# Two layers of cross-attention on one core: VectorE's and ScalarE's order written out by hand

## The chip, the core and the metric

The kernel runs on one NeuronCore of a Trainium2 chip. The metric is the device time of one execution in microseconds (us). TensorE (PE) multiplies matrices and transposes, VectorE (DVE) and ScalarE (ACT) work on what it leaves in PSUM, GpSimd (POOL) adds in SBUF and issues DMAs of results, SyncE (SP) issues the loads. All arithmetic is in float32.

## The reference, cut to what matters

Two layers follow one another. For each of 8 images there are 100 queries of 640 channels (20 heads of 32 channels), 77 text tokens and 645 image tokens of 1024 channels.

```
layer 0:  q = x Wq;  k, v = text Wk, text Wv;  k_ip, v_ip = ip Wk_ip, ip Wv_ip
          out = softmax(q k / sqrt(32)) v + softmax(q k_ip / sqrt(32)) v_ip      (each head)
          x1  = out Wo + bo + x
layer 1:  the same with its own weights, but
          sem  = (softmax over text of q k_text, all 640 channels) text . ip / sqrt(32)
          ip probabilities = softmax(scores_ip + 0.5 sem) * mask of the query
          result = out Wout + bout + x1
```

A layer of an image is called a unit u (0 to 15; layer 1 from 8 on), four heads of a unit are a chunk c (0 to 4), so there are 80 chunks in all, listed in ORDER.

## The kernel before, in words

**First part (to about 200 us).** Queries of layer 0, keys and values of the text and of the last five image tokens are made and written to DRAM.

**Second part (200 to 2070 us).** Two streams of work are interleaved by hand.

The first stream makes keys and values of the image tokens for two images at once (a pair of units; pair_tasks, and for the last pair two_chunks and fifth_chunk). Matrices are multiplied in the manner of Strassen, with seven products in place of eight: `seven` (L179) gives seven steps, first, sixth, second, seventh, fifth, fourth, third. Each step is one product on PE into a PSUM bank (psv_a to psv_e for values, psk_a to psk_e for keys, psvk_a to psvk_e for the last pair) and then an instruction that takes it out: a copy by ACT (L193, L202) or an addition by DVE (L198, L208, L213, L219, L224). There are two banks for it (ps_pj). Sums of tokens that the products need come from DVE (token_sums, L231; third_sum, L527; L725 and L726 in the last pair), sums of weights too (weight_sums, L127, four additions L134 to L137; `asked` spreads them as tasks, in the first pair two of the four run on POOL). `last_k` is the plain product for the fifth group of keys.

The second stream is the attention of the chunks. For a chunk, `scores` (L934) with part 0 makes scores with 512 keys and with part 1 those with 210 keys. Both parts use one PSUM tile, sc, of four banks, one for each head. DVE takes the maxima (L953; in layer 1 L960, with the semantic scores added), ACT the exponentials (L968), DVE the text maxima and differences (L974 to L980), ACT their exponentials (L983, L984), DVE the factors (L985 to L991), and then the probabilities are scaled: 512 columns by ACT (L997), the rest by DVE (L1001, L1005). What can wait is put in the list `later` in portions, and `emit(n)` takes n of them. A portion marked True has to be out before the score tile is used again (free_scores, L928).

One chunk later, `transposes` (L1021) turns the probabilities on PE in six groups, pspt, four heads each; DVE copies groups 0, 1, 3 and 4 (L1037), ACT groups 2 and 5 (L1035). `values` (L1040) multiplies with the values (pv) and DVE copies the result (hs, L1056). Two PSUM banks (ps_pt) are shared by pspt, pv and by all small work of a chunk: out_piece (pso L858, taken out by DVE at L863), q_piece (psq, by ACT at L881), and for layer 1's semantic scores sem_text (L831, ACT L833), sem_logits (L805, DVE L810, ACT L811, DVE L812 and L813), sem_transpose (L818, ACT L820) and sem_scores (L840, ACT L841).

**The order of the work.** `production` lists the first stream's tasks with a cost each (0 for sums and loads) and `spread` gives each a place between chunks. The loop over ORDER at the end goes through a chunk so: score product part 0; tasks and small work; transposes 0 and 1 of the chunk before; tasks and small work; transposes 2 and 3; score product part 1; tasks and small work; transposes 4 and 5; tasks and small work; the values of the chunk before. `between` (L1240) runs the tasks that are due and the small work, `apart` sees to it that there is a product between two things that use the same banks where one is to be had, and `next_task` (L1220) runs one task and, if it had a cost, emits one portion. `small_work` (L1148) says which small work a chunk has.

The loop stands in a block in which PE runs its instructions in the order in which the program gives them:

```
with tc.manual_schedule(engines={mybir.EngineType.PE}):
```

The order on the other engines is chosen by the compiler's scheduler, from the dependences and its own estimate of times.

Of the kernel before, what the change touches and what calls it, by code (L numbers as in the profile page):

```python
# [9 lines left out]
F32 = mybir.dt.float32  # L10
AF = mybir.ActivationFunctionType
ALU = mybir.AluOpType
AX = mybir.AxisListType

P = 128
# [29 lines left out]
def two_layer_xattn(  # L45
# [654 lines left out]
    def last_visits(visits):  # L700

        xs, lists = {}, []
        for i, (j, tasks_of) in enumerate(visits):

            def begin(i=i):
                if i == 0:
                    xs.update(places[LAST])
                elif i + 2 < len(visits):
                    xs[i + 2] = load_x(LAST, visits[i + 2][0])

            lists.append([(0.0, begin)] + tasks_of(j, xs, i))
        return lists

    def two_chunks(r, j, xs, at):
        n0, n1 = BLOCKS[j]
        n = n1 - n0
        sums, o, made, late = {}, {}, {}, []

        def begin():
            t = spool.tile([P, 3, HK, 2, NX], F32, tag="s", name=f"sl_{r}_{j}")  # L720
            a11, a12, a21, a22 = quarters(xs[at], n)
            s1, s2, s4 = (t[:, i, :, 0, :n] for i in range(3))
            sums.update(token_sums(a11, a12, a21, a22, s1, s2, None, s4))
            sums[7] = a21
            late.append(lambda: nc.vector.tensor_tensor(a21, a11, a21, ALU.subtract))  # L725
            late.append(lambda: nc.vector.tensor_tensor(s4, a12, s2, ALU.subtract))  # L726
            o[0] = opool.tile([P, 2, 2, P + NX], F32, tag="made", name=f"vko_{r}_{j}")

        def product(ps, which, go_on):
            for k in range(HK):  # L730
                nc.tensor.matmul(
                    ps[:, :P], lhsT=sums[which][:, k, :P], rhs=W["v", WHICH[which]][:, k, r * P : (r + 1) * P],
                    start=(k == 0 and not go_on), stop=(k == HK - 1), skip_group_check=True,
                )
            for k in range(HK):
                nc.tensor.matmul(
                    ps[:, P : P + n], lhsT=W["k", WHICH[which]][:, k, r * P : (r + 1) * P], rhs=sums[which][:, k, :],
                    start=False, stop=(k == HK - 1), skip_group_check=True,
                )

        def step(i):
            if i == 0:
                made[0] = seven(
                    f"psvk_{r}_{j}", product, tuple(o[0][:, h, m, : P + n] for h in range(2) for m in range(2))
                )
            made[0][i]()
            if i < 6:
                return
            for h, u in enumerate(LAST):
                nc.gpsimd.dma_start(  # L750
                    k_d[u][:, :4, n0:n1].rearrange("p (m r) n -> p r m n", r=2)[:, r], o[0][:, h, :, P : P + n]
                )
                nc.gpsimd.dma_start(
                    v_d[u][j * P : (j + 1) * P, : 4 * P].rearrange("p (m r n) -> p r m n", m=2, r=2)[:, r],
                    o[0][:, h, :, :P],
                )

        steps = [(1.8, lambda i=i: step(i)) for i in range(7)]
        sums_ = [(0.0, lambda i=i: late[i]()) for i in range(2)]
        return [(0.0, begin)] + steps[:1] + sums_[:1] + steps[1:4] + sums_[1:] + steps[4:]  # L760

    def fifth_chunk(kinds, j, xs, at):
        n0, n1 = BLOCKS[j]
        tasks = []
        for kind in kinds:
# [28 lines left out]
                        nc.gpsimd.dma_start(v_d[u][j * P : (j + 1) * P, 4 * P :], t[:, i, :P])  # L794

            tasks += [(1.8, lambda h=h, f=half: f(h)) for h in range(2)]
        return tasks


    sem_state, gs = {}, {}  # L800
# [125 lines left out]
    def emit(n):  # L926
        for _ in range(n):
            later.pop(0)[1]()  # L928

    def free_scores():  # L930

        emit(max([i + 1 for i, (r, _) in enumerate(later) if r], default=0))

    def scores(u, c, part):  # L934
        k0, k1 = ((0, KA), (KA, NK))[part]
        free_scores()
        if part == 0:
            pr[u, c] = ppool.tile([S, 4, NK], F32, tag="p", name=f"p_{u}_{c}")

            stats[u, c] = stat.tile([S, 14, 4], F32, tag="st", name=f"st_{u}_{c}")  # L940
        sc = ps_sc.tile([P, 4, 512], F32, tag="sc", name=f"sc_{u}_{c}_{part}")
        for i in range(4):
            rows = slice(32 * i, 32 * i + 32)
            nc.tensor.matmul(  # L944
                sc[:S, i, : k1 - k0], lhsT=qs_[u][rows, c, :], rhs=ks[u, c][rows, k0:k1], start=True, stop=True
            )
        p, st, l = pr[u, c], stats[u, c], u // B
        n = min(k1, NI) - k0
        lo, f, rz, mul = st[:, 6, :], st[:, 7:9, :], st[:, 9:11, :], st[:, 11:13, :]

        def maxima(heads):
            if l == 0:
                nc.vector.tensor_reduce(  # L953
                    st[:, part, heads[0] : heads[-1] + 1], sc[:S, heads[0] : heads[-1] + 1, :n], AX.X, ALU.max,
                    negate=True,
                )
                return
            for i in heads:

                nc.vector.tensor_tensor_reduce(  # L960
                    out=p[:, i, k0 : k0 + n], in0=sc[:S, i, :n], in1=sems[u][:, k0 : k0 + n], scale=-1.0,
                    scalar=3.0e38, op0=ALU.add, op1=ALU.min, accum_out=st[:, part, i : i + 1],
                )

        def exponentials(heads):
            for i in heads:
                dst = p[:, i, k0 : k0 + n]
                nc.scalar.activation(  # L968
                    dst, dst if l else sc[:S, i, :n], AF.Exp, bias=st[:, part, i : i + 1],
                    scale=-1.0 if l else 1.0, accum_out=st[:, 3 + part, i : i + 1],  # L970
                )

        def text_maxima():
            nc.vector.tensor_reduce(st[:, 2, :], sc[:S, :, n:KB], AX.X, ALU.max, negate=True)  # L974

            nc.vector.tensor_tensor(
                p[:, :, NI:], sc[:S, :, n:KB], st[:, 2, :].unsqueeze(2).to_broadcast([S, 4, NT]), ALU.add
            )
            nc.vector.tensor_tensor(lo, st[:, 0, :], st[:, 1, :], ALU.min)
            nc.vector.tensor_tensor(f, lo.unsqueeze(1).to_broadcast([S, 2, 4]), st[:, 0:2, :], ALU.subtract)  # L980

        def text_exponentials():
            nc.scalar.activation(f, f, AF.Exp)  # L983
            nc.scalar.activation(p[:, :, NI:], p[:, :, NI:], AF.Exp)  # L984
            nc.vector.tensor_reduce(st[:, 5, :], p[:, :, NI:], AX.X, ALU.add)  # L985
            nc.vector.tensor_tensor(st[:, 3:5, :], st[:, 3:5, :], f, ALU.mult)
            nc.vector.tensor_tensor(st[:, 4, :], st[:, 3, :], st[:, 4, :], ALU.add)

        def factors():
            nc.vector.reciprocal(rz, st[:, 4:6, :])  # L990
            nc.vector.scalar_tensor_tensor(  # L991
                mul, f, mask_sb[:, l : l + 1], rz[:, 0:1, :].to_broadcast([S, 2, 4]), ALU.mult, ALU.mult
            )

        def scaled(heads):
            for i in heads:
                nc.scalar.activation(p[:, i, :KA], p[:, i, :KA], AF.Copy, scale=mul[:, 0, i : i + 1])  # L997

        def scaled_rest(text):
# [4 lines left out]
            else:  # L1004
# [2 lines left out]
                    ALU.mult,  # L1007
                )

        if part == 0:  # L1010
            maxima((0, 1))
            later.append((True, lambda: (exponentials((0, 1)), maxima((2, 3)))))
            later.append((True, lambda: exponentials((2, 3))))
        else:
            maxima((0, 1, 2, 3))
            later.append((True, lambda: (exponentials((0, 1, 2, 3)), text_maxima())))
            later.append((False, text_exponentials))
            later.append((False, lambda: (factors(), scaled((0, 1)), scaled_rest(False))))
            later.append((False, lambda: (scaled((2, 3)), scaled_rest(True))))

    pts = {}  # L1021

# [38 lines left out]
    def production():  # L1061
# [44 lines left out]
        for kinds, js in (("kv", every[:2]), ("k", every[2:]), ("v", every[2:])):  # L1106
            visits += [(j, lambda j, xs, i, kinds=kinds: fifth_chunk(kinds, j, xs, i)) for j in js]
        lists = last_visits(visits)
        lists[0][1:1] = v_last[2:3]
        lists[0][3:3] = v_last[3:]  # L1110
        for a, b, tasks in (
            (n - 10 - AHEAD, n + 2.9, lists[: 2 * NB]),
            (n + 2.9, n + 6.9, lists[2 * NB : 3 * NB]),
# [94 lines left out]
        if n == len(ORDER) - 4:  # L1208
            last_out_weights()

    with tc.manual_schedule(engines={mybir.EngineType.PE}):
        for _, f in pair_tasks(PAIRS[0]):
            f()
        load_q(0)
# [3 lines left out]
        done = [0]  # L1218

        def next_task():  # L1220
            todo[done[0]][2]()
            if todo[done[0]][0] and later:
                emit(1)
            done[0] += 1

        def make(until):
# [13 lines left out]
        def between(n, a, b, small):  # L1240

            mark[0] = done[0]
            near = 0.4 if n < NC_ * LAST[0] + 6 else 0.1
            for i, (_, f) in enumerate(small):
                make(n + a + (b - a) * (i + 1) / (len(small) + 1))
                apart(n + b + near)
                f()
            make(n + b)
            apart(n + b + near)
# [86 lines left out]
```

## Time and profile before

| | us |
|---|---|
| median of 3 runs | 2071.68 (2071.6 to 2073.09) |
| the profiled execution | 2071.6 |
| its span, first to last instruction | 2069.8 |
| PE busy | 2043.5 |
| PE's weight loads busy (beside PE) | 1581.2 |
| DVE busy | 1074.8 |
| ACT busy | 799.6 |
| POOL busy | 309.9 |
| mean granted clock of TensorE | 0.998 |

A line of the profile's groups has the line of the kernel, the engine, the operation, what it writes and reads, and counts and times. In a list of waits the numbers after the colon are the total in us, how often, and the longest. In a timeline the first number is the start in us from the span's start, the second the time that the merged instructions took, and a bracket gives the idle time of the engine before it and what ended that. A matmul on float32 shows as two instructions, so a product of four matmuls has x8.

By stretches of the span, the busy times of PE, DVE and ACT are:

| stretch, us | PE, of the stretch | DVE | ACT |
|---|---|---|---|
| 212 to 400 | 188.0 of 188 | 48.1 | 15.2 |
| 600 to 800 | 199.6 of 200 | 104.8 | 81.9 |
| 1000 to 1200 | 193.6 of 200 | 114.9 | 81.4 |
| 1600 to 1800 | 197.3 of 200 | 127.0 | 94.2 |
| 1800 to 1900 | 99.6 of 100 | 77.4 | 59.9 |
| 1900 to 2000 | 97.7 of 100 | 72.2 | 61.4 |
| 2000 to 2070 | 62.6 of 70 | 47.5 | 46.9 |

### The profile page before, as it was taken

Reading aid. Unit: us, or ns where it says so; the run is one execution under the profiler, and the core shown is the slowest. Engines: PE = TensorE matmul, PEld = TensorE weight load, DVE = VectorE, ACT = ScalarE, POOL = GpSimd, SP = SyncE. Lnnn points to the kernel's source line nnn. Section 1 sums busy time; section 2 is a strip of 40 time slices with the busy share of each in tenths; the row PEclk is TensorE's granted clock in tenths of the full one; section 3 lists DMA queues with packets and bytes.
Section 4 is the critical chain, followed back from the end, with each engine's and each line's share of the span. In section 5 each row is a group of like instructions: output and inputs, shape, how many; then the busy total and the mean of one; then the engine's idle time right before and its main releaser. Section 6 shows DMA issues by size and latency. Waiting matters only on the chain.

```text
span 2069.8 us, 38196 instructions
## 1 busy us (share of the span) xinstructions
PE 2043.5 (99%) x15122; PEld 1581.2 (76%) x15122; DVE 1074.8 (52%) x2789; ACT 799.6 (39%) x2271; POOL 309.9 (15%) x445
## 2 busy tenths in 40 slices
PE   9999999999999999999989999999999999999998
PEld 8676767677778777786778777787778778889787
DVE  2211322355554655455475555455555557777676
ACT  1001000244433434344333444435444445565576
POOL 3212312111111111010110111010111111111120
PEclk9999999999999999999999999999999999999999
DMA  9545313232424433262543533262434345545472
GB/s 327 155 132 171 97 56 105 88 107 71 129 83 131 129 113 91 81 179 65 160 133 103 147 105 106 72 178 75 115 89 134 90 133 151 158 133 140 121 211 74
DMA packets 302544, 255.35 MB, mean 123 GB/s; under 512 B 46686, under 2 KB 271378, under 8 KB 302366
## 3 DMA queue, kind: packets, MB, share of 16 engines
q1 hardware_dynamic: 280590, 184.48, 32.2%
q0 software_dynamic: 21776, 68.44, 9.5%
q8 instruction: 119, 1.95, 0.4%
q14 instruction: 59, 0.48, 0.1%
HBM read 183.93 MB, written 68.93 MB: 122 GB/s over the span
## 4 chain that ended last, share of the span: by engine, by line
PE 95%; DVE 2%; DMA 1%; ACT 1%; issue 1%; POOL 0%; SPq 0%; ACTq 0%; DVEq 0%
PE psv_a L597 8%; PE psv_d L597 8%; PE pspt L1030 8%; PE psk_d L625 6%; PE psk_a L625 6%; PE sc L944 6%; PE psk L563 5%; PE psv_e L597 4%; PE pv L1052 4%; PE psv_c L597 4%; PE psv_b L597 4%; PE psk_e L625 3%; PE psk_c L625 3%; PE psk_b L625 3%; PE pso L858 3%; PE psq L275 2%
## 5 line engine op out<-in xcount | busy, mean ns | idle before, releaser
L968 ACT ACTIVATE p<-sc,st 100x512 f32<-100x512 f32 (+1 forms) x320 | 166.4, 528 | 218.5 <-DVE st L953 218.2
L1037 DVE COPY pt<-pspt 128x400 f32<-128x400 f32 x319 | 175.5, 569 | 122.8 <-PE pspt L1030 116.6
L997 ACT ACTIVATE p<-p,st 100x512 f32<-100x512 f32 x320 | 208.5, 713 | 62.8 <-DVE st L991 62.7
L968 ACT ACTIVATE p<-p,st 100x512 f32<-100x512 f32 (+1 forms) x320 | 177.1, 555 | 132.3 <-DVE st L960 131.8
L1030 PEld LDWEIGHTS pspt<-ident,p 100*128 100x128 f32 (+1 forms) x1920 | 188.0, 137 | 42.1 <-issue 5.0
L1030 PE MATMUL pspt<-ident,p 100*128 100x100 f32 (+1 forms) x1920 | 211.0, 250 | 5.7 <-DVE res L863 2.4
L597 PE MATMUL psv_a<-wv,x 128*128 128x397 f32 (+1 forms) x560 | 185.0, 472 | 1.3 <-ACT vo L193 1.3
L646 POOL DMA_DIRECT2D k_d<-ko x140 | 99.5, 715 | 527.6 <-DVE ko L219 470.9
L597 PE MATMUL psv_d<-wv,s 128*128 128x320 f32 (+1 forms) x560 | 174.9, 455 | 0.0
L1035 ACT COPY pt<-pspt 128x400 f32<-128x400 f32 (+1 forms) x161 | 78.4, 487 | 227.7 <-PE pspt L1030 227.3
L953 DVE TENSOR_REDUCE st<-sc 100x2 f32<-100x1024 f32 (+1 forms) x120 | 126.3, 1052 | 59.4 <-ACT p L968 30.5
L597 PEld LDWEIGHTS psv_a<-wv,x 128*128 128x128 f32 x560 | 103.5, 190 | 63.7 <-issue 8.1
L960 DVE CUSTOM_DVE_ANT_0 p<-sc,sem 100x512 f32<-100x512 f32 (+1 forms) x320 | 139.7, 489 | 22.5 <-PE sc L944 22.3
L597 PEld LDWEIGHTS psv_d<-wv,s 128*128 128x128 f32 x560 | 103.4, 190 | 57.4 <-issue 5.5
L625 PE MATMUL psk_a<-x,wk 128*128 128x256 f32 (+1 forms) x672 | 137.2, 350 | 4.2 <-ACT ko L193 4.2
L944 PE MATMUL sc<-k,q 32*100 32x210 f32 (+1 forms) x1280 | 138.6, 502 | 0.8 <-ACT p L968 0.6
L625 PE MATMUL psk_d<-s,wk 128*128 128x256 f32 (+1 forms) x672 | 136.4, 348 | 0.0
L612 POOL DMA_DIRECT2D v_d<-vo x70 | 38.3, 548 | 642.4 <-DVE gst L587 317.5
L563 PE MATMUL psk<-x,wk 128*128 128x256 f32 (+1 forms) x560 | 132.0, 383 | 0.0
L625 PEld LDWEIGHTS psk_a<-x,wk 128*128 128x128 f32 x672 | 110.8, 192 | 24.7 <-issue 6.0
L563 PEld LDWEIGHTS psk<-x,wk 128*128 128x128 f32 x560 | 102.8, 189 | 25.7 <-issue 9.9
L625 PEld LDWEIGHTS psk_d<-s,wk 128*128 128x128 f32 x672 | 108.3, 189 | 17.5 <-issue 5.2
(209 smaller groups left out, 3234.5 us busy)
## 6 DMA issues: line engine op xcount, KB each, us to landing
x<-ip_t SPq DMA_DIRECT2D x84, 512.0 KB
k<-k_d SPq DMA_DIRECT2D x80, 322.5 KB
v<-v_d SPq DMA_DIRECT2D x80, 320.0 KB
v_d<-vo POOLq DMA_DIRECT2D x70, 320.0 KB, 2.5
k_d<-ko POOLq DMA_DIRECT2D x112, 128.0 KB, 4.3
x<-ip_t SPq DMA_DIRECT2D x22, 532.0 KB
o<-wo SPq DMA_DIRECT2D x35, 320.0 KB
q<-wq SPq DMA_DIRECT2D x20, 320.0 KB
```

Source lines behind the costliest of these rows:

```text
L563: nc.tensor.matmul(ps[:, : 2 * n], lhsT=W["k", 4][:, k, :], rhs=x_all[:, at[j], :, k, :n], start=(k == 0), stop=(k == NCC - 1),)
L597: nc.tensor.matmul(ps[:, :m], lhsT=tokens(k)[:, :P], rhs=w[:, k, :], start=(k == 0 and not go_on), stop=(k == HK - 1), skip_group_check=True,)
L625: nc.tensor.matmul(ps[:, i * m : (i + 1) * m], lhsT=W["k", WHICH[which]][:, k, r * P : (r + 1) * P], rhs=tokens(k), start=(i == 0 and k == ...
L646: nc.gpsimd.dma_start(dst[:, :, r], ko[0][:, h, :, i, p0 : p0 + n])
L944: nc.tensor.matmul(sc[:S, i, : k1 - k0], lhsT=qs_[u][rows, c, :], rhs=ks[u, c][rows, k0:k1], start=True, stop=True)
L953: nc.vector.tensor_reduce(st[:, part, heads[0] : heads[-1] + 1], sc[:S, heads[0] : heads[-1] + 1, :n], AX.X, ALU.max, negate=True,)
L960: nc.vector.tensor_tensor_reduce(out=p[:, i, k0 : k0 + n], in0=sc[:S, i, :n], in1=sems[u][:, k0 : k0 + n], scale=-1.0, scalar=3.0e38, op0= ...
L968: nc.scalar.activation(dst, dst if l else sc[:S, i, :n], AF.Exp, bias=st[:, part, i : i + 1], scale=-1.0 if l else 1.0, accum_out=st[:, 3 ...
L997: nc.scalar.activation(p[:, i, :KA], p[:, i, :KA], AF.Copy, scale=mul[:, 0, i : i + 1])
L1030: nc.tensor.transpose(ps[:rows, i * S : (i + 1) * S], pr[u, c][:, i, j * P : j * P + rows], ident[:S, :S])
L1037: nc.vector.tensor_copy(dst, src)
L1052: nc.tensor.matmul(ps[32 * i : 32 * i + 32, :S], lhsT=lhs, rhs=pt[:rows, j, i * S : (i + 1) * S], start=(j == 0), stop=(j == 5),)
```

## The change

1. The block in which the order is the program's now holds for DVE and ACT as well as for PE.
2. The score tile of four banks becomes two tiles of two banks (sc0 with heads 0 and 1, sc1 with heads 2 and 3), both from the same pool.
3. The maxima of all four heads are asked for right after the score product. In part 1 the text maxima, the text's additions (both now for two heads at a time) and the differences follow them at once, where before they came after the exponentials.
4. The portions in `later` are cut differently. Part 0 has the exponentials of heads 0 and 1 and those of heads 2 and 3. Part 1 has all exponentials with the text's; the factors with the rest of the scaling by DVE; the scaling of heads 0 and 1 with the text's; the scaling of heads 2 and 3.
5. `next_task` emits a portion ahead of a task with a cost instead of behind it. `between` emits a portion ahead of each piece of small work. Part 0 of a chunk emits all that is left.
6. In the last pair, the token sums of a list of steps run in one task with the last step of the list before. The last two of its weight sums stand behind its second and third step instead of ahead of its first.

```diff
-            lists.append([(0.0, begin)] + tasks_of(j, xs, i))
+            first_sums, tasks = tasks_of(j, xs, i)
+            if first_sums and i:
+                t, f = lists[-1][-1]
+                lists[-1][-1] = (t, lambda f=f, g=first_sums: (f(), g()))
+            lists.append([(0.0, begin)] + ([(0.0, first_sums)] if first_sums and not i else []) + tasks)
...
-        free_scores()
         if part == 0:
+            emit(len(later))
...
+        else:
+            free_scores()
-        sc = ps_sc.tile([P, 4, 512], F32, tag="sc", name=f"sc_{u}_{c}_{part}")
+        scs = [ps_sc.tile([P, 2, 512], F32, tag=f"sc{h}", name=f"sc_{u}_{c}_{part}_{h}") for h in range(2)]
...
+        for h in range(2):
+            maxima(h)
         if part == 0:
-            maxima((0, 1))
-            later.append((True, lambda: (exponentials((0, 1)), maxima((2, 3)))))
-            later.append((True, lambda: exponentials((2, 3))))
+            later.append((True, lambda: exponentials(0)))
+            later.append((True, lambda: exponentials(1)))
         else:
-            maxima((0, 1, 2, 3))
-            later.append((True, lambda: (exponentials((0, 1, 2, 3)), text_maxima())))
-            later.append((False, text_exponentials))
-            later.append((False, lambda: (factors(), scaled((0, 1)), scaled_rest(False))))
-            later.append((False, lambda: (scaled((2, 3)), scaled_rest(True))))
+            for h in range(2):
+                text_maxima(h)
+            differences()
+            later.append((True, lambda: (exponentials(0), exponentials(1), text_exponentials())))
+            later.append((False, lambda: (factors(), scaled_rest(False))))
+            later.append((False, lambda: (scaled((0, 1)), scaled_rest(True))))
+            later.append((False, lambda: scaled((2, 3))))
...
-        lists[0][1:1] = v_last[2:3]
-        lists[0][3:3] = v_last[3:]
+        lists[0][5:5] = v_last[2:3]
+        lists[0][7:7] = v_last[3:]
...
-    with tc.manual_schedule(engines={mybir.EngineType.PE}):
+    with tc.manual_schedule(engines={mybir.EngineType.PE, mybir.EngineType.DVE, mybir.EngineType.Activation}):
...
         def next_task():
-            todo[done[0]][2]()
             if todo[done[0]][0] and later:
                 emit(1)
+            todo[done[0]][2]()
             done[0] += 1
...
                 apart(n + b + near)
+                if later:
+                    emit(1)
                 f()
```

`differences` holds the two small operations that were at the end of text_maxima, and the three small operations that were at the end of text_exponentials (the text's sum and the product and sum of the two parts' sums) are now at the head of `factors`.

## The prediction

> **What bounds the kernel now.** I read the page first, then PE's waits, then the timeline around them. Page, busy time by engine and chain by engine:
>
> ```profile
> PE 2043.5 (99%) x15122; PEld 1581.2 (76%) x15122; DVE 1074.8 (52%) x2789; ACT 799.6 (39%) x2271; POOL 309.9 (15%) x445
> PE 95%; DVE 2%; DMA 1%; ACT 1%; issue 1%; POOL 0%; SPq 0%; ACTq 0%; DVEq 0%
> ```
>
> PE is the bound from end to end. Only its stalls can be won: 2069.8 - 2043.5 = 26 us without a matmul, part of it fixed (4.5 us for the first load). Busy PE isn't always PE at its pace, so I also took the time from each product's first matmul to the next one's: an 8-matmul product of 320 columns has 2.15 us nearly everywhere, one of 256 columns 1.73. Summed over all products, what exceeds the usual by over 0.15 us is 28 us. Where it sits (PE's waits):
>
> ```profile
> PE psk_a L625 <- ACT ko L193: 4.2, 1, 4.2
> PE pspt L1030 <- DVE res L863: 2.4, 11, 0.6
> PE psk_c L625 <- DVE ko L198: 1.5, 1, 1.5
> PE psv_a L597 <- ACT vo L193: 1.3, 1, 1.3
> ```
>
> Three single long waits, and one short wait that comes back with every pair's output pieces. The timeline shows what is behind the longest:
>
> ```profile
> 1032.29 1.12 PE L944 MATMUL sc<-k,q 32*100 32x512 f32 x8
> ...
> 1037.67 1.49 DVE L134 TENSOR_TENSOR wvt<-wv,wv 128x1280 f32<-128x1280 f32 x1 [4.98 <-DMA wv<-wvi]
> 1039.08 1.22 DVE L953 TENSOR_REDUCE st<-sc 100x2 f32<-100x1024 f32 x1
> ...
> 1041.01 0.37 ACT L193 COPY ko<-psk_a 128x266 f32<-128x266 f32 x1
> ...
> 1041.43 3.62 PE L625 MATMUL psk_a<-x,wk 128*128 128x133 f32 x16 [4.19 <-ACT ko L193]
> ```
>
> The scores were there at 1033.4, but DVE stood before a weight sum (L134) whose load hadn't landed; the maxima (L953) came 5.7 us late, the exponentials after them, and ACT's copy out of psk_a's bank behind the exponentials. In program order that sum stands six steps later.
>
> [...] 4.98 us of idle DVE with ready work in its queue. The forecast goes by this, in both directions: the pinned order takes such a case away and can make others. [...] after the 4.2 us stall, matmuls of psk_a start 222 ns apart instead of 113, and the stretch 1032 to 1044.8 has a granted clock of 0.87, so 12.8 x 0.13 = 1.7 us lost. I count it with the stall.
>
> **The change part by part.** The sum is against the profiled execution, 2071.6 us (span 2069.8, 1.8 around it); the median is 2071.68, so no correction. PE's order was pinned before and hardly changes. A chunk is one image's four heads; T is the start of its first score product (512 keys), T2 of its second (210 keys).
>
> *1. DVE and ACT in program order: weight sums no longer run ahead.* The 4.2 us and their 1.7 of half clock go; so do 1.4 at 1063 (psv_b took 3.6 for 2.15: four sums of wk, 1.22 each, between the maxima) and 1.6 at 1723 (psk_a 3.5 for 1.8, sums of wv). -8.9. In program order the same sums stand between products one by one. PE wants a product's bank back two products later, so an addition (0.45) may be late by a product less itself, 1.75 - 0.45 = 1.3 us, and a sum takes 1.22; the loads, issued from 1026 on, have landed by then: 0. The two last sums (v_last), moved behind the second and third step of the last pair's first list, are needed by its fifth and sixth: 0. The first pair's sums move too, behind seven products; POOL's half (4.2 + 3.1 us) then runs beside additions that read PSUM, which kept 0.49 us beside POOL at 91.7 and 359: 0.
>
> *2. All maxima at once, two score tiles.* Part 0: two reduces of 1.22 us end at T+3.6 (layer 1: four of 0.61). An addition of the first product behind them ends at T+4.1; PE wants that bank after two products, at T + 1.05 + 2 x 1.75 = 4.6 at the earliest: covered by 0.5. Exponentials end by T+5 instead of after the first product's addition; small stalls on them (0.8 at 1165, 0.3 each at 692 and 927) go: -1.5 (0 to -3). Part 1: the text maxima and additions are four instructions of some 0.32 (0.47 for 308 columns is 0.16 fixed + 1.0 ns each) instead of 0.47 + 0.48: DVE +0.33 us a chunk, +0.5 with the split reduce. Hidden wherever a chunk has 16 us or more.
>
> *3. Portions asked for ahead of the small work.* This is what I weigh most. Today, in the chunk at 648:
>
> ```profile
> 648.15 0.61 PE L944 MATMUL sc<-k,q 32*100 32x210 f32 x8
> 648.69 2.00 PE L625 MATMUL psk_e<-x,wkt 128*128 128x256 f32 x8
> 650.53 1.85 PE L858 MATMUL pso<-hs,o 128*128 128x200 f32 x10
> 652.16 0.46 ACT L984 ACTIVATE p<-p 100x308 f32<-100x308 f32 x1 [0.96 <-DVE p L976]
> 652.42 0.43 DVE L863 SCALAR_TENSOR_TENSOR res<-pso,bias_sb,res 128x200 f32<-128x200 f32 x1 [0.22 <-PE pso L858]
> 652.90 0.54 PE L1030 MATMUL pspt<-ident,p 100*82 100x100 f32 x4 [0.17 <-DVE res L863]
> 653.26 0.47 DVE L985 TENSOR_REDUCE st<-p 100x4 f32<-100x308 f32 x1
> ...
> 654.52 0.71 DVE L1005 TENSOR_TENSOR p<-p,st 100x532 f32<-100x532 f32 x1
> ```
>
> The sixth transpose needs the bank that the output piece holds, so it waits for L863. In the new order psk_e's step takes the first portion and the output piece the second: factors and the scaled rest. DVE's queue is then: two maxima (start T2+0.68 as here, 0.35 apart), two text maxima and two additions (0.24 to 0.37 each with the wait on one another), the two small differences, end T2+3.05; psk_e's addition to 3.45; L985, which waits for ACT. ACT has the four exponentials by T2+2.7, then waits for the differences and has the text exponential at T2+3.75. L985 to L991 take 1.25 us here, L1005 0.63, and only then comes L863: T2+5.7 to 6.1. The transpose starts at T2+6.2 instead of 4.75: +1.45. PE's order has six chunks in which no product stands between that piece and the transposes (those that begin at 632, 867, 1107, 1336, 1775 and 1943; the one at 1564 has a product): **+8.7**. The same for the logits of the semantic scores (layer 1, whose exponentials end 0.25 later): L810 starts at T2+5.95, L811 frees the bank at 6.65, and PE is at the sixth transpose at T2+5.45 in four of seven chunks (+1.2 each), at 6.2 in two (+0.45), at 3.6 in the one near 1821 (+2.4): **+8.0**. Bounds: 0, if DVE were through with the portion before the piece ends, and +22 for both, if the exponentials end 0.4 us later than I put them (13 places).
>
> *4. Small copies on ACT behind the exponentials.* sem_text's and sem_transpose's copies now follow both pairs of exponentials (layer 1: 1.95 to 5.0 after T, a copy out of psum 0.4); in the chunks near 1631, 1743, 1810, 1828, 1890, 1909, 1925 PE wants the bank at T + 5.1 to 5.5: +0.5 each, +3 (0 to +6).
>
> *5. Last pair.* Its sums follow the third step in one task: DVE 1.4 us ahead of the transposes' copies, and ahead of the next x load on SP (a load for two lists later: it isn't awaited); POOL's writes wait for the third step's addition as before. The short chunks (12.4 us, as 1762 to 1774) hold on DVE: maxima 2.45 + 0.87, text 0.95, factors 1.5, rest 1.2, copies 2.3 + 0.26, additions 1.3, sums 1.6 = 12.4. It is full, and 0.33 comes on top; +0.4 in some eight of them: +3 (0 to +6).
>
> *6. Tail.* Chunks after 2012 have no product between parts; there the exponentials move behind the sixth transpose's copy, and the stall of 0.9 before pv goes: +1 (-2 to +4).
>
> Sum: -8.9 - 1.5 + 8.7 + 8.0 + 3 + 3 + 1 = +13.3: **2085 us**.
>
> **Rivals.** (a) The sums of step 1 go and the cover of step 3 holds. It is decided at one point: whether L863 starts before T2+4.3. For: ACT is busy 39%, and DVE 52%. Against: L985 follows L984 by 0.6 us even now, and L863 stood ahead of it. -10.4 + 3 = 2064. It ends faster. (b) Half of step 3, 4 to 6: the exponentials end earlier, or the order isn't held where I read it: -10.4 + 11 = 2072. (c) In the last pair's short chunks DVE's queue never catches up and the lag passes from chunk to chunk: 20 chunks at 1 us more, and one or two half-clock windows of 1.7: 2071.6 + 13 + 15 = 2100.
>
> **How the numbers follow.** A measurement of this kernel tells 0.2% (4 us) from no change. Chances: forecast 0.52 (own range 2077 to 2094), (a) 0.24, (b) 0.12, (c) 0.12. So slower 0.64, same 0.12, faster 0.24. The range reaches into (a) and (c) and leaves out about a tenth on each side: 2060 to 2098.
>
> **What would show it.** Step 1: no wait of psk_a for L193, and 1.00 as granted clock from 1000 to 1100. Step 3: PE's waits list pspt <- DVE res with some 10 us in 6 to 11 waits of up to 2, and pspt <- ACT tp with 7; in the timeline L985 and the 532-column product stand ahead of res. Step 5: more DVE waits at L1030 after 1740. I am wrong if DVE res stays at 2.4 us (then (a)), or if the loss lies in ordinary chunks, between 430 and 620, where I expect none.

## The result, and the profile after

The changed kernel takes 2090.71 us (median of 5 runs, 2089.93 to 2091.22) against 2071.6 (5 runs, 2068.57 to 2073.09): ratio 1.0096, 95% interval 1.0082 to 1.011. The forecast was 2085.0 with its own range 2077 to 2094, so side and range hold, and it was 5.7 us short. The profiled execution has 2091.22 and a span of 2089.5, 19.7 more than before.

From the page of the changed kernel, the busy time by engine, and then lines of PE's list of waits:

```profile
PE 2051.0 (98%) x15122; PEld 1585.3 (76%) x15122; DVE 1096.1 (52%) x2989; ACT 791.4 (38%) x2271; POOL 310.3 (15%) x445
```

```profile
PE pspt L1043 <- DVE res L868: 10.9, 11, 1.9
PE pspt L1043 <- ACT tp L816: 7.3, 6, 2.7
...
PE pspt L1043 <- DVE pt L1050: 2.6, 2, 2.3
PE psvk_b L736 <- DVE sl L233: 2.5, 1, 2.5
```

The line numbers have moved: L863 is now L868, L810 and L811 are L815 and L816, L953 is L961, L985 is L997, L997 is L1007, L1030 and L1037 are L1043 and L1050. The two waits that step 3 named stand on top, with the sums it gave them (10 and 7). The third line is a wait that step 4 brings, below. The three long single waits of before (psk_a, psk_c, psv_a) are gone. PE is busy 7.5 us longer for the same 15122 matmuls; an estimated 6.8 us of it are half clock, also below.

Timeline of the changed kernel where the 4.2 us stall was:

```profile
1036.77 1.12 PE L952 MATMUL sc<-k,q 32*100 32x512 f32 x8
...
1037.92 2.36 DVE L961 TENSOR_REDUCE st<-sc 100x2 f32<-100x1024 f32 x2 [0.75 <-PE sc L952]
...
1041.56 1.99 PE L625 MATMUL psk_a<-x,wk 128*128 128x133 f32 x16
```

No weight sum stands ahead of the maxima any more. They start as the scores end (1036.77 + 1.12 = 1037.89), and psk_a's second product follows without a wait.

Timeline of the changed kernel in the chunk that the prediction shows at 648 (T2 is 647.68):

```profile
650.05 1.85 PE L863 MATMUL pso<-hs,o 128*128 128x200 f32 x10
...
651.78 0.47 DVE L997 TENSOR_REDUCE st<-p 100x4 f32<-100x308 f32 x1 [0.92 <-ACT p L994]
...
653.06 0.71 DVE L1015 TENSOR_TENSOR p<-p,st 100x532 f32<-100x532 f32 x1
653.69 0.42 DVE L868 SCALAR_TENSOR_TENSOR res<-pso,bias_sb,res 128x200 f32<-128x200 f32 x1
...
654.16 0.54 PE L1043 MATMUL pspt<-ident,p 100*82 100x100 f32 x4 [1.91 <-DVE res L868]
```

The factors and the 532-column product now precede the piece's addition. That starts at T2+6.01 (forecast 5.7 to 6.1), and the transpose that waits for it at T2+6.48 (forecast 6.2). The piece itself was through on PE at 651.9.

To place the whole difference I measured each chunk from its first score product to the next one's, in both traces (the last one to the end of its last product). Most of the 80 agree to 0.1 us. The ones that don't fall under the steps of the prediction. Chunk 58 is shared out by the experiments below: of its +4.1 us, 3.5 go with step 3's two lines, and the +0.6 that stay are step 1's.

| step | forecast | after - before, us | where |
|---|---|---|---|
| 1, weight sums | -8.9 | -7.1 | chunk 28 -6.0, chunk 29 -1.7, chunk 58 +0.6 (-1.7 for the old stall, +2.3 for a new one) |
| 2, maxima | -1.5 | -1.7 | chunks 13, 23, 33, 53 and 61 |
| 3, output piece | +8.7 | +11.0 | chunks 11, 21, 31, 41, 61, 71 |
| 3, logits | +8.0 | +12.1 | chunk 58 +3.5, chunk 63 +5.0; 38, 48 and 68 +0.9 to +1.3; two others +0.1 |
| 4, small copies on ACT | +3 | +3 | chunk 70 +1.75, the rest 0.7 or less |
| 5, last pair full | +3 | +0.4 | chunk 66 alone |
| 6, tail | +1 | +2.4 | chunks 77 and 78 |
| none, the time to the first chunk | 0 | -0.5 | two executions of the changed kernel are 0.9 apart there, so it is no effect |
| sum | +13.3 | +19.6 | the span has +19.7 |

Part of this is the clock. The first rows are windows around stalls of the changed kernel in chunks 58, 63 and 70, the others are the kernel before in chunks 70 and 63. In each row the third number from the end is the granted clock, the share of TensorE's full clock:

```profile
1741.00:1749.00 8.00, 5.50 (x72) 4.71 (x74) 4.79 (x9) 2.81 (x6) 0.00 (x0) 0.79 0.23 62
1831.00:1845.00 14.00, 11.29 (x112) 10.00 (x111) 7.89 (x25) 6.37 (x16) 1.77 (x3) 0.76 0.51 132
1946.00:1960.00 14.00, 11.29 (x109) 7.48 (x107) 7.78 (x30) 7.60 (x23) 0.92 (x2) 0.76 0.22 62
```

```profile
1930.00:1944.00 14.00, 12.36 (x129) 8.84 (x128) 9.98 (x33) 7.18 (x24) 2.00 (x3) 0.88 0.34 100
1825.00:1839.00 14.00, 14.00 (x165) 12.53 (x164) 12.04 (x40) 8.59 (x24) 2.84 (x4) 1.00 0.48 129
```

Length times missing clock estimates the loss: 8 x 0.21 + 14 x 0.24 + 14 x 0.24 = 8.4 us here in the changed kernel, 14 x 0.12 = 1.7 before. With a stretch at 655.4 the changed kernel loses 10.2 us to half clock ahead of its end, the kernel before 3.4 (at 1041 and 1939).

### The profile page after: what moved, and what is told of

It is laid out like the page before. It is cut to its first block, busy times and chain, and to the rows that moved or that the text cites. A ratio compares the mean times of both kernels' runs of the same rounds, so it can differ in the third digit from the quotient of the medians.

```text
span 2089.5 us, 38492 instructions
## 1 busy us (share of the span) xinstructions
PE 2051.0 (98%) x15122; PEld 1585.3 (76%) x15122; DVE 1096.1 (52%) x2989; ACT 791.4 (38%) x2271; POOL 310.3 (15%) x445
## 5 line engine op out<-in xcount | busy, mean ns | idle before, releaser
L1050 DVE COPY pt<-pspt 128x400 f32<-128x400 f32 x319 | 175.5, 569 | 135.8 <-PE pspt L1043 133.0
L1043 PE MATMUL pspt<-ident,p 100*128 100x100 f32 (+1 forms) x1920 | 214.1, 251 | 24.2 <-DVE res L868 10.9
L1043 PEld LDWEIGHTS pspt<-ident,p 100*128 100x128 f32 (+1 forms) x1920 | 188.7, 137 | 62.8 <-DVE res L868 12.9
L1007 ACT ACTIVATE p<-p,st 100x512 f32<-100x512 f32 x320 | 208.1, 714 | 42.4 <-DVE st L1001 42.3
L967 DVE CUSTOM_DVE_ANT_0 p<-sc,sem 100x512 f32<-100x512 f32 (+1 forms) x320 | 138.8, 491 | 24.3 <-PE sc L952 24.2
L961 DVE TENSOR_REDUCE st<-sc 100x2 f32<-100x1024 f32 (+1 forms) x160 | 125.3, 825 | 30.7 <-PE sc L952 30.7
L625 PEld LDWEIGHTS psk_a<-x,wk 128*128 128x128 f32 x672 | 109.2, 189 | 20.4 <-issue 6.0
```

Source lines behind the costliest of these rows:

```text
L625: nc.tensor.matmul(ps[:, i * m : (i + 1) * m], lhsT=W["k", WHICH[which]][:, k, r * P : (r + 1) * P], rhs=tokens(k), start=(i == 0 and k == ...
L961: nc.vector.tensor_reduce(st[:, part, 2 * h : 2 * h + 2], scs[h][:S, :, :n], AX.X, ALU.max, negate=True)
L967: nc.vector.tensor_tensor_reduce(out=p[:, i, k0 : k0 + n], in0=scs[h][:S, i % 2, :n], in1=sems[u][:, k0 : k0 + n], scale=-1.0, scalar=3.0e ...
L1043: nc.tensor.transpose(ps[:rows, i * S : (i + 1) * S], pr[u, c][:, i, j * P : j * P + rows], ident[:S, :S])
L1050: nc.vector.tensor_copy(dst, src)
```

## The experiments

The theory was that the order of step 3 (portions asked for ahead of the small work, with DVE and ACT held to it) makes the loss, and that the pinned order alone makes the gain. The rivals: that the pin costs by itself, or the other edits, or the last pair.

### No portion ahead of small work

```diff
                 apart(n + b + near)
-                if later:
-                    emit(1)
                 f()
```

> The changed kernel without the emission ahead of small work; all else of the change stays. Theory (the factors and the scaled rest stand ahead of the output piece's and the logits' instruction on VectorE): the waits pspt for res fall from 10.9 to about 2.4 us, those for tp from 7.3 to about 2, and with the shorter stalls most of the half-clock windows go (20 us of them cost 10 now, 7 before): 2090.7 - 9 - 8 - 6 = about 2067. Rival (the pinned order itself, or a VectorE that is full in the last pair, makes the loss): 2083 or more, with the waits moved elsewhere.

Measured 2070.32 us, ratio 0.9995 [0.9986, 1.0003]: 20.4 us less than the changed kernel, for two lines. PE's waits of this kernel:

```profile
PE pspt L1043 <- DVE res L868: 1.7, 10, 0.2
...
PE pspt L1043 <- ACT tp L816: 1.2, 2, 0.8
```

Both waits of step 3 fall to about what they were before (2.4 and 0.4), so those two lines make them. The time stays some 3 us above expectation: the last chunk takes 26.34 us for the 22.8 of before, since with no task left in it the portions there came only with the transposes. The kernel with portions in the last chunk only, below, takes that up.

### Only DVE and ACT pinned

The kernel before with the engines' set of the changed one, and nothing else:

```diff
-    with tc.manual_schedule(engines={mybir.EngineType.PE}):
+    with tc.manual_schedule(engines={mybir.EngineType.PE, mybir.EngineType.DVE, mybir.EngineType.Activation}):
```

> The kernel before with the pinned order of VectorE and ScalarE alone; no other edit. Theory (pinning puts the weight sums back in their places, and in the order of before the output piece stands ahead of the text's exponentials and factors): 9 to 10 us less than before, minus 0 to 6 for copies that stand behind exponentials: 2062 to 2068. Rival (pinning is what costs): 2080 or more.

Measured 2131.98 us, ratio 1.0292 [1.0278, 1.0306]: a clear miss. Chunks 28 and 29 gain 6.0 and 1.1 us as foreseen, but chunks 71 to 79 lose 50.6. PE's waits, and the timeline in one of these chunks:

```profile
PE pspt L1030 <- ACT p L997: 29.6, 49, 3.0
```

```profile
1980.22 0.09 DVE L960 DVE_READ_ACCUMULATOR2_ANT st<- 100x1 f32 x1
...
1981.31 0.19 DVE L990 RECIPROCAL st<-st 100x8 f32<-100x8 f32 x1
...
1981.85 1.33 ACT L997 ACTIVATE p<-p,st 100x512 f32<-100x512 f32 x2 [7.68 <-DVE st L991]
...
1982.62 0.30 PE L1030 MATMUL pspt<-ident,p 100*128 100x100 f32 x1 [1.71 <-ACT p L997]
```

The factors (L990) of the chunk before stand behind the next chunk's first maxima (L960) on DVE; ACT idled 7.68 us for them. So the order that the old code writes down is a bad one, which the scheduler had hidden on DVE and ACT. About half of the 50.6 us is not wait but clock: from chunk 71 on the same 1350 matmuls keep PE busy 144.3 us for 119.4, at a mean granted clock of 0.88. The pin alone isn't the gain: it needs portions cut for it.

### The changed kernel with only PE pinned

The same line, turned round in the changed kernel.

> The changed kernel with only TensorE's order pinned. Theory: the scheduler is free to move res and sst ahead of the factors, so the 11 + 7 us of waits go, and the weight sums run ahead again as before (+9): 2068 to 2076. Rival (the split score tiles and the cut portions make the loss, whoever orders them): 2085 to 2095.

Measured 2081.62 us, ratio 1.0048 [1.0035, 1.006], above what was expected. Chunks 28 and 29 gain only 1.2 and 0.5 us: the weight sums run ahead again (psk_c waits 5.1 us for DVE ko, in two waits). The output piece's wait is 6.9 us, the longest 1.2, for 10.9 and 1.9: the scheduler mends part of the order, not all. So the gain of step 1 does come from the pin, and the loss of step 3 from where the portions are asked for, more so with the pin. The time is between theory (2068 to 2076) and rival (2085 to 2095): the theory had the scheduler mend all of it.

### Only exponentials ahead of small work

```diff
-                if later:
+                if later and later[0][0]:
```

> As the changed kernel, but ahead of small work only exponentials are emitted (portions marked True), the factors not. Theory: pieces and logits as in the run without any emission, while the small copies of ScalarE still stand behind the exponentials: 0 to 4 us above that run, about 2069. Rival (the exponentials ahead of small work are what delays the pieces): no gain over the changed kernel's 2090.7.

Measured 2073.33 us, ratio 1.0013 [1.0005, 1.0021]; the two waits are 1.9 and 1.2. It differs from the kernel without portions there by exponentials alone and takes 3.0 us more, in chunks 63 (+1.0 against before) and 70 (+1.75). That is step 4, and 17.4 of the 20.4 us are the factors and the rest of the scaling, step 3. In both kernels a loss of 3.5 us in the last chunk stands against these gains, which the next kernel takes away.

### Portions ahead of small work in the last chunk only

```diff
-                if later:
+                if later and n == len(ORDER) - 1:
```

> The changed kernel, with the emission ahead of small work kept for the last chunk alone. Theory: the last chunk has no products, so there the emission is what brings its exponentials forward; without it that chunk took 26.3 us instead of 22.9. With it back: 2070.3 - 3.4 = 2067. Rival (the last chunk's loss came from something else): 2070.

Measured 2066.52 us, ratio 0.9972 [0.996, 0.9983]. The last chunk is back at 22.9 us. The change without the portions of steps 3 and 4 is 24.2 us faster than with them, and 5 faster than the kernel before.

### The last pair's first weight sums earlier

On top of that, the sums L134 and L135 five and four tasks ahead of the fifth keys, in place of one and none:

```diff
-... ("k 4", 1, v_last[:1]), ("k 4", 0, v_last[1:2]))
+... ("k 4", 5, v_last[:1]), ("k 4", 4, v_last[1:2]))
```

> As the run with the emission in the last chunk alone, and the first two weight sums of the last pair moved four steps forward, behind the second and third step of the keys before them. Theory: the 2.2 us that the sixth product of the last pair's first list waits for its token sums come from a weight sum in front of them on VectorE; they go, and part of the 0.8 of the logits: 2 us less, 2065. Rival (the token sums wait for the last product that reads their buffer, whatever stands on VectorE): no difference.

Measured 2064.23 us, ratio 0.9961 [0.9947, 0.9975]. The reason for it is the changed kernel's timeline in chunk 58:

```profile
1736.65 1.22 DVE L134 TENSOR_TENSOR wvt<-wv,wv 128x1024 f32<-128x1024 f32 x1
...
1740.03 0.23 DVE L815 TENSOR_REDUCE sst<-psm 100x1 f32<-100x77 f32 x1
...
1740.76 0.54 PE L1043 MATMUL pspt<-ident,p 100*82 100x100 f32 x4 [1.41 <-ACT tp L816]
...
1741.12 1.22 DVE L135 TENSOR_TENSOR wvt<-wvt,wv 128x1024 f32<-128x1024 f32 x1
...
1742.97 0.69 DVE L233 TENSOR_TENSOR sl<-sl,x 128x512 f32<-128x512 f32 x1
...
1743.81 1.61 PE L736 MATMUL psvk_b<-wvt,sl 128*128 128x128 f32 x8 [2.50 <-DVE sl L233]
```

L134 stands ahead of the logits' reduce, and L135 ahead of the token sums that psvk_b's product reads. Moved forward, the wait of psvk_b falls from 2.2 us (the kernel above) to 0.2, and chunk 58 takes 21.95 us for 23.99 without the edit and 23.38 in the kernel before. What step 1 put at 0, "in program order the same sums stand between products one by one", was wrong for these two.

### A portion behind a task with a cost

The kernel of the last chunk only, with next_task's portion behind the task again:

```diff
-            if todo[done[0]][0] and later:
-                emit(1)
             todo[done[0]][2]()
+            if todo[done[0]][0] and later:
+                emit(1)
```

> As the run with the emission in the last chunk alone, but portions are emitted behind a product's addition again, as before the change. Theory (the 60 us that the pinned order alone lost in the last chunks come from portions behind additions that wait for TensorE): the time goes up, most of it in chunks 71 to 79: 2085 to 2120. Rival (they come from the old cut, in which maxima of heads 2 and 3 and the text's maxima stand behind exponentials): about 2067 to 2072.

Measured 2071.35 us, ratio 0.9996 [0.9988, 1.0004]: the time is the rival's, and the theory falls. A portion ahead of a product rather than behind it is worth 4.8 us, in chunks 58, 63, 64, 66, 76 and 78 (0.7 to 1.6 each), and the 60 us of pinning alone don't follow from it. That they come from the old cut isn't shown by this, since all else here is the new one; the pinned kernel with a flush, below, goes back to it.

### The changed kernel once more

> The changed kernel once more, for a second profile. The stalls should be the same to 0.1 us, chunk by chunk. If the half clock depends on where a stall lies against a window that runs by itself, the half-clock stretches are at other chunks and sum up to something other than 20 us; if it depends on the length of the stall alone, they are at the same chunks.

One execution, 2088.99 us. Every chunk with a stall of step 3 comes out the same to 0.1 us, but for chunk 11, which takes 29.68 us where it took 31.35. Windows of both executions, the first profile and then this one:

```profile
640.00:660.00 20.00, 18.09 (x102) 16.07 (x101) 8.91 (x26) 5.79 (x17) 2.85 (x4) 0.91 0.30 87
```

```profile
640.00:660.00 20.00, 18.09 (x152) 15.87 (x150) 9.22 (x26) 6.16 (x18) 3.40 (x5) 1.00 0.36 100
```

The same 1.9 us wait for L868 lies in both; half clock followed in one (20 x 0.09 = 1.8 us). The later stretches at half clock come back in both (mean granted clock 0.995 and 0.996). So 1.7 of the 11.0 us of the output pieces are chance.

### Pinned, and what is put off asked for ahead of a chunk's scores

The pinned kernel before, and in `scores`:

```diff
-        free_scores()
         if part == 0:
+            emit(len(later))
+        else:
+            free_scores()
+        if part == 0:
             pr[u, c] = ...
```

> The kernel before with DVE and ACT in program order, as in e3_pin_only, and one thing more: whatever is still put off of the chunk before (sums, factors, scaling) is asked for ahead of a chunk's first scores. Our theory of e3: its 60 us come from the factors of the chunk before, which there stand behind the maxima of the next chunk on DVE, so that the portions of ACT and with them the transposes come late in the last pair. It expects chunks 71 to 79 to lose at most 12 us instead of 50, the transposes' wait for ACT's scaled p to fall from 29.6 to under 5 us, and 2068 to 2085 us in all. The rival: the maxima in two halves, of which the second stands behind exponentials, hold the transposes up in program order whatever comes first; then chunks 71 to 79 still lose over 30 us and the time stays above 2110.

Measured 2090.65 us, ratio 1.0087 [1.0071, 1.0103]: 41 us back, and still 5.7 above the range. Chunks 71 to 75 lose 2.6 us for 23.5, so put-off work behind the next maxima, the factors among it, is shown to be what held those. Chunks 76 to 79 still lose 16.4 (27.1). So chunks 71 to 79 lose 19 us where the theory allowed 12 and the rival asked for over 30, and the wait for ACT's scaled p is 7.5 us, not under 5. PE's waits, and a window at its end:

```profile
PE pspt L1033 <- ACT p L1000: 7.5, 19, 2.5
...
PE sc L947 <- DVE p L979: 2.6, 2, 1.3
```

```profile
2064.00:2089.00 25.00, 17.40 (x185) 14.60 (x183) 7.84 (x23) 6.65 (x18) 0.00 (x0) 0.70 0.06 21
```

25 x 0.30 = 7.5 us of the 16.4 are half clock (the kernel before has 0.99 there), behind waits that remain. The maxima in two halves and the single score tile (the wait of sc for L979) are left as their likely source, since the kernel with a portion behind a task, which has neither, loses 4.1 in these chunks. But the two also differ in how the portions are cut and in what the last chunk asks for. Which of these it is stays open.

### What is put off asked for ahead of the values, in the last four chunks

On top of the earlier sums:

```diff
             if last:
+                if n >= len(ORDER) - 4:
+                    emit(len(later))
                 values(*last)
```

> e7_sums_early, and in the last four chunks what is still put off is asked for ahead of the product of p and v, so that on DVE the factors no longer stand behind the copy of that product. Our theory: that copy's place is what is left of the loss in chunks 77 and 78 (1.0 and 1.3 us over the kernel before); it expects both back to the kernel before's within 0.3 us and 2062 us, 1.0 to 2.5 under e7_sums_early. The rival: in these chunks the exponentials start too late on ACT for the order on DVE to matter; then chunks 77 and 78 stay as they are and the time is that of e7_sums_early, 2064.

Measured 2062.48 us, ratio 0.9955 [0.9942, 0.9968]. Chunk 77 loses 0.37 us against the kernel before where it lost 1.02, chunk 78 0.68 (1.33), and chunk 79 gains 0.33 on the earlier sums' kernel. The wait in these chunks falls from 1.5 us in 5 waits to this, PE's waits from 1998 on:

```profile
PE pspt L1043 <- ACT p L1007: 0.5, 2, 0.3
```

The order on DVE is about half of the tail's loss; the other half, which the theory also gave to it, stays, so the expected 0.3 us is missed. The 1.75 us between the two medians agrees with the 1.6 of these chunks, but the two intervals overlap. This is the fastest kernel of the case, 9 us under the kernel before and 28 under the changed one.

## Why the prediction was right, and where it was off

**Step 1** held in cause and place, and came out 1.8 us short (-7.1 for -8.9): the pinned orders of two different kernels both have the 6.0 us of chunk 28, the unpinned one 1.2. Its "0" for the sums in program order failed in chunk 58, by 2.3 us, of which 2.0 go when two sums are moved: the working put a sum between two additions, and left out that a reduce of the logits and the token sums of the next step stood behind it.

**Step 2** held in size (-1.7 for -1.5). What the sum did not show is how much the pin leans on the other edits: pinned without them the kernel before is 60 us slower, and the flush at a chunk's start gives back 41 of these. The four text instructions took 0.31 to 0.32 us each at 154 columns, as worked out; in the trace of before DVE's TENSOR_TENSOR on 4 or 8 columns takes 0.16 us, and its reduces 0.24 on 77 columns, 0.47 on 308 and 1.22 on 1024.

**Step 3** is the loss, as weighed. The stalls were sized well: for the output pieces about 9.3 (8.7 forecast), for the logits 7.0 (8.0), which is their 12.1 less the 5.1 of half clock in chunks 58 and 63; the wait for ACT tp grew by 6.9. Removing the two lines removes both. The working by queue order was right to 0.3 us in the chunk shown.

**The mis-sized term is the clock.** Step 1 counted 1.7 us of half clock with the old stall, but step 3 priced its new stalls as waits alone. Ahead of its end the changed kernel has four such stretches, 20.5 us long in all, for 3.4 that the forecast left standing: 17.1 x 0.5 = 8.5 us, about 1.7 with the output pieces, 3.4 with the logits of chunk 63, 1.7 with step 4, and 1.7 in chunk 58, where the logits' wait and the token sums' wait of step 1 stand close together. That is more than the whole miss. The profile before had the warning: the stretch that was left standing, 1930 to 1944 at 0.88, comes without any wait of PE over 0.64 us near it.

**Step 4** has its 3 us, partly by luck. Not seven places lose 0.5 each: in chunk 70 one wait has 2.3 us (pspt for DVE pt, the third line of PE's list), chunks 63 and 69 have 0.7 and 0.5. The small copy of sem_transpose (L825) does stand behind the exponentials there and ends only at 1953.54, where in the kernel without portions ahead of small work it runs at once and the transposes follow without a wait. Here they start at 1953.36, released by DVE's copy L1050 out of the other bank. About 1.7 of the 3 us are again the clock.

**Step 5** failed: the short chunks 60, 62, 65, 67 and 72 take the same time to 0.1 us. Its 3 us, which never came, stand against the clock's 8.5 in the sum: without them the forecast would have been over 8 us short, so the nearness of the total is luck in part. "It is full" was a sum of durations from several places, 12.4 of 12.4 us. DVE's row over the short chunk that it named, first in the kernel before, then in the changed one (busy time after the chunk's length, DVE alone in the first, third of the five engines in the second):

```profile
1762.11:1774.52 12.41, 9.94 (x35) 1.00 0.38 102
```

```profile
1767.54:1779.96 12.42, 12.42 (x164) 10.96 (x152) 9.90 (x36) 6.66 (x22) 0.00 (x0) 1.00 0.30 76
```

DVE had 2.5 us to spare before the change. Not every chunk has every item of the sum.

**Step 6** was +2.4, inside its range; half of it is DVE's order there.

**The rivals.** (a) fell: L868 starts at T2+6.0, not before 4.3. (b) fell: step 3's stalls came in full. (c) fell in its place, since the short chunks lose nothing, though its half-clock windows came, from step 3's stalls. Its number doesn't follow from its terms either: 20 chunks at 1 us and one or two windows of 1.7 are 22 to 23 us, not 15. That no ordinary chunk lost between 430 and 620 was as forecast: PE's waits from 400 to 1700 are the output pieces and the logits alone.

## What to carry to other kernels

When an engine's order is pinned, the order written in the program becomes a cost (60 us in the kernel that was pinned and nothing else): before pinning, read for each bank that the bound engine wants back what stands ahead of the instruction that frees it, and ask for that instruction first. Work that is merely put off (factors, scaling) belongs ahead of a long product that covers it, not ahead of a short piece whose bank the next instruction needs (17.4 us here). Price a stall of TensorE as its wait plus what the clock may take afterwards (1.7 us here after a wait of 1.9, in one execution of two), and don't read an effect of 2 us from one profile of each kernel.

## What the runs showed of the hardware

A half-clock stretch has a granted clock of 0.50 (655.44 to 658.85 in the changed kernel) and is not tied to the end of a stall: that one starts 1.28 us after its stall ended (654.16), the one at 1833.04 starts 0.80 us before its stall ends (1833.84). In the changed kernel all ahead of its end are 3.413 us long or twice that, and their starts lie 319.0, 345.0 and 380.0 times 3.413 us after the first; in the kernel before the two ahead of its end are 3.413 us long and 263.0 times that apart. So within each of these executions they stand on a fixed grid of time.

A stall of 1.9 us brought half clock on in one execution (0.91 from 640 to 660) and none in the next (1.00). Cut into windows of the grid's length, the first execution has the whole stall in one of them; the second has it split over two, with 1.6 and 0.3 us. The window that holds most of it, first execution and second:

```profile
652.03:655.44 3.41, 1.50 (x12) 1.20 (x11) 2.80 (x9) 0.70 (x2) 0.56 (x1) 1.00 0.60 173
```

```profile
649.55:652.96 3.41, 1.79 (x13) 1.56 (x11) 2.36 (x9) 1.28 (x8) 1.43 (x2) 1.00 0.39 103
```

PE was busy for 1.50 us of the one and 1.79 of the other. That this made the difference is not shown, and busy time alone doesn't decide it: in the changed kernel the window at 1949.09, also with 1.79 us, was followed by half clock, and the one at 890.96 with 1.74 us was not; in the kernel before the one at 1935.49 with 2.41 us was. What sets these apart is not shown either.

Equal waits can differ by 2.2 us in what the clock takes: in chunk 70 the kernel with the earlier sums and the one with put-off work ahead of the values have the same code and three waits of PE of the same lengths (0.6, 0.5 and 0.4 us), but from 1916 to 1940 one has a granted clock of 0.86 and the other 1.00, and the chunk takes 18.20 us in one and 15.99 in the other.
